# Layer 2 as seven block products before the mixing, and another order of the first gathers, in a four-layer graph network on one core

## The chip, the cores and the metric

The kernel runs on one core of one Trainium2 chip. Times are device microseconds (us) of one launch. Every ratio to the kernel before is between executions on the same chip in the same call; where a run is compared with the changed kernel or with another run, the two come from different calls, and between these the median of the kernel before went from 3187.1 to 3191.3 us. A ratio is the mean time of one kernel's fast runs over the mean of the other's of the same rounds, so it is not quite the ratio of the medians that are quoted. The profile is one execution, with times of each engine's instructions: PE is TensorE (matmul), DVE VectorE, ACT ScalarE, POOL GpSimd, SP SyncE. "Clock" is the share of full speed that TensorE's throttle granted.

## The reference

Input x is 128 batches of 128 nodes by 256 features, fp32; adj is a sparse 128 by 128 matrix. Four graph layers follow each other, each with a residual and a layer normalization:

```python
x = layernorm(x + attention_over_edges(x))          # layer 0: gathers, segment softmax, scatter
h = relu(Wt @ (x @ W1)); h = relu(Wt @ (h @ W2))    # layer 1, Wt = adj * adj
x = layernorm(x + Wt @ (h @ W3))                    #   widths 256, 512, 1024, 256
h = einsum('bjf,kfo->kbjo', x, W)                   # layer 2: three products 256 -> 256
x = layernorm(x + diag(adj) @ h[0] + triu(adj, 1) @ h[1] + tril(adj, -1) @ h[2] + bias)
x = layernorm(x + batchnorm2(relu(batchnorm1(A_hat @ x @ W1.T)) @ W2.T))   # layer 3 [cut]
```

Layer 2 may mix the nodes first and multiply by W afterwards, or the other way round. Mixing only acts on the nodes and W only on the features, so the results agree.

## The kernel before

A "quad" is four batches; 32 quads pass through a software pipeline. One iteration works on layer 2 and 3 of quad a = k-1, layer 1's second product of c = k, layer 1's start of b = k+1, the attention of e = k+2 and the queries of g = k+3. The schedule is written by hand: the program sets the order of each engine's work. The big products (layer 0's values, layer 1's first and second, layer 3's hidden) already use Strassen's scheme in Winograd's form: seven block products instead of eight, with sums of blocks on VectorE.

Layer 2 of one quad mixed each batch first (split_t holds the two triangles) and then made six matmuls of 256 columns per batch:

```python
def mix(i):                                   # [cut: allocation]
    for dc in range(DC):
        nc.tensor.matmul(pm[:, dc]..., s.xr[:, i, dc * P:(dc + 1) * P], split_t..., start=True, stop=True)
    nc.scalar.copy(ms[:, 1:3]..., pm)
    for dc in range(DC):
        nc.tensor.transpose(pt[:, dc, :], s.xr[:, i, dc * P:(dc + 1) * P], ident)
    nc.vector.tensor_mul(ms[:, 0], pt, diag_bc...)
def prod(i):
    for n3, (t, dc) in enumerate((t, dc) for t in range(3) for dc in range(DC)):
        nc.tensor.matmul(po[:, i % 2, :], mss[i][:, t, dc, :], l2w[:, t, dc, :],
                         start=(n3 == 0), stop=(n3 == 3 * DC - 1))
    if i % 2:
        nc.vector.tensor_add(xj, s.xb[:, i - 1:i + 1, :], po)     # residual; layer_norm(xj) later
```

One stretch is `second`, layer 1's second product of quad c. It has fourteen places at which other work can be hung in (`after(i)` runs what the schedule put at place i):

```python
product(y, 0, "A11", B11); keep(p1, 0, "p1"); after(0)
product(y, 1, "A11", B11); keep(p1, 1, "p1"); after(1)
product(x, 0, "A12", B21); total(0, 0, 0, x, p1); after(2)
product(z, 0, "S1", T1);   after(3)
product(y, 0, "S2", T2);   keep(u2, 0, "u2"); after(4)   # keep: ScalarE copies the bank
product(y, 1, "S2", T2);   keep(u2, 1, "u2"); relu(0, 0, 0); after(5)
product(x, 1, "A12", B21); total(1, 0, 0, x, p1); after(6)
product(y, 0, "S3", T3)    # accumulates into y[0]: only after the copy u2 has read it
# [cut: seven more products of this kind, up to after(13)]
```

The layer normalization takes statistics on VectorE (`ln_st`, `ln_mv`), a square root on ScalarE (`ln_sd`) and the rest on VectorE.

## Time and profile before

| | before |
|---|---|
| time, median of 3 (later 4) runs | 3188.79 us (3187.04 to 3189.34) |
| profiled span | 3186.6 us |
| TensorE, VectorE, ScalarE busy | 98%, 68%, 41% |
| period of one quad | 86.92 us |
| granted TensorE clock, whole span | 0.992 |

The prediction below shows the lines behind these numbers. One view it tells only in a sum is the list of what TensorE waited for (engine, what it wanted, who released it and where: total us, times, longest). The largest entries of the kernel before are:

```profile
PE py L443 <- ACT adc L429: 8.8, 1, 8.8
PE pt L1372 <- ACT agg L1214: 7.6, 4, 3.3
```

One happens once, the other four times. No entry happens once per quad: in the steady part there is no wait to remove.

### The profile page before, as it was taken

How to read it: one execution, taken by the hardware profiler on the slowest of the kernel's cores; microseconds unless marked ns; L12 is line 12 of the kernel's file. 1: busy time of each engine (PE TensorE's matmuls, PEld its weight loads, DVE VectorE, ACT ScalarE, POOL GpSimd, SP SyncE). 2: the span in 40 equal slices, each digit the busy share in tenths (PEclk: the TensorE clock that was granted, in tenths of full speed). 3: DMA queues.
4: the chain of work that ended last, by engine and by line, in shares of the span. 5: the costliest groups of instructions: out<-in, count | busy, mean ns of one | idle time of the engine just before them, and what ended most of it. 6: DMA issues, size and time to landing. Idle time of an engine off the chain costs nothing. (4 is left out here: it accounts for less than half of the span.)

```text
span 3186.6 us, 40910 instructions
## 1 busy us (share of the span) xinstructions
PE 3119.4 (98%) x15651; PEld 2574.5 (81%) x15651; DVE 2162.4 (68%) x4209; ACT 1311.9 (41%) x2359; POOL 649.2 (20%) x533
## 2 busy tenths in 40 slices
PE   7899999999999999999999999999999999999997
PEld 3788888888888888888888888888888888874444
DVE  6676666666767676666666767676666666438888
ACT  3344333334433434333334433433333333326668
POOL 3211222212211211222212211211222211001135
PEclk8899999999999999999999999999999999999999
DMA  7422333333333322333333333323333321005457
GB/s 210 132 73 81 100 107 100 107 92 102 107 95 98 100 86 80 100 106 100 106 90 103 107 91 102 98 86 82 100 106 100 105 84 51 21 27 193 175 199 266
DMA packets 117459, 340.12 MB, mean 107 GB/s; under 512 B 14864, under 2 KB 51600, under 8 KB 108944
## 3 DMA queue, kind: packets, MB, share of 16 engines
q0 software_dynamic: 44400, 147.35, 19.0%
q1 hardware_dynamic: 71104, 189.23, 16.4%
q8 instruction: 124, 2.03, 0.3%
q10 hardware_dynamic: 1760, 0.92, 0.1%
q14 instruction: 71, 0.58, 0.1%
HBM read 252.00 MB, written 85.46 MB: 106 GB/s over the span
## 5 line engine op out<-in xcount | busy, mean ns | idle before, releaser
L643 PE MATMUL p<-w,h 128*128 128x256 f32 x2048 | 464.7, 380 | 0.0
L562 PE MATMUL ph<-m,w 128*128 128x256 f32 x2048 | 463.0, 379 | 0.0
L643 PEld LDWEIGHTS p<-w,h 128*128 128x128 f32 x2048 | 389.8, 190 | 67.0 <-issue 8.3
L562 PEld LDWEIGHTS ph<-m,w 128*128 128x128 f32 x2048 | 386.8, 190 | 51.4
L331 POOL DMA_INDIRECT zs<-qd,src_idx x122 | 118.3, 970 | 1407.8 <-DMA qd<-qt 829.0
L562 PE MATMUL ph<-m,w_s 128*128 128x256 f32 x1536 | 354.4, 380 | 0.0
L693 PE MATMUL po<-l2w,ms 128*128 128x256 f32 x1536 | 347.5, 379 | 1.2 <-DVE ms L685 1.2
L562 PEld LDWEIGHTS ph<-m,w_s 128*128 128x128 f32 x1536 | 292.9, 191 | 40.2
L693 PEld LDWEIGHTS po<-l2w,ms 128*128 128x128 f32 x1536 | 284.4, 190 | 36.2 <-DVE ms L685 1.5
L113 ACT ACTIVATE ln_sd<-ln_mv,eps 128x2 f32<-128x2 f32 x192 | 56.2, 293 | 499.5 <-DVE ln_mv L108 499.5
L331 POOL DMA_INDIRECT zs<-qd,dst_idx x122 | 207.6, 1701 | 244.1 <-DMA zs<-qd,src_idx 236.2
L414 POOL DMA_INDIRECT attd<-at,att_idx x128 | 127.8, 998 | 300.6 <-DMA attd<-at,att_idx 239.3
L569 ACT COPY u<-ph 128x512 f32<-128x512 f32 x128 | 75.0, 586 | 247.6 <-PE ph L562 247.6
L575 DVE TENSOR_TENSOR h<-ph,u 128x512 f32<-128x512 f32 x128 | 88.2, 689 | 109.7 <-ACT u L569 58.1
L366 DVE TENSOR_TENSOR zs<-zs,a_bc 128x1024 f32<-128x1024 f32 x125 | 153.1, 1225 | 4.3
L367 DVE TENSOR_REDUCE scores<-zs 128x16 f32<-128x1024 f32 x125 | 152.5, 1220 | 4.3
L681 ACT COPY ms<-pm 128x512 f32<-128x512 f32 x128 | 71.2, 581 | 200.0 <-PE pm L679 200.0
L364 DVE SCALAR_TENSOR_TENSOR zs<-zs 128x1024 f32<-128x1024 f32 x125 | 152.1, 1217 | 1.3 <-DMA zs<-qd,dst_idx 1.3
L504 DVE TENSOR_TENSOR h<-z,adc 128x512 f32<-128x512 f32 x62 | 41.8, 674 | 156.5 <-ACT adc L498 156.5
L106 DVE BATCH_NORM_STATS2 ln_st<-xr 128x6 f32<-128x256 f32 x384 | 144.2, 418 | 5.5
L121 DVE TENSOR_SCALAR xr<-xr,ln_mv,ln_rs 128x256 f32<-128x256 f32 x384 | 142.6, 414 | 6.9
L667 POOL TENSOR_TENSOR xb<-xr,bias 128x512 f32<-128x512 f32 x64 | 81.5, 1273 | 298.3 <-DVE xr L121 159.3
(304 smaller groups left out, 5701.7 us busy)
## 6 DMA issues: line engine op xcount, KB each, us to landing
ad<-attd SPq DMA_DIRECT2D x32, 1024.0 KB, 4.8
zd<-z SPq DMA_DIRECT2D x31, 1024.0 KB, 7.4
zl<-zd SPq DMA_DIRECT2D x62, 512.0 KB, 3.5
xr<-in_x_dram SPq DMA_DIRECT2D x32, 512.0 KB, 5.9
x3d<-xr SPq DMA_DIRECT2D x32, 512.0 KB, 2.9
x3l<-x3d SPq DMA_DIRECT2D x32, 512.0 KB, 5.1
out_dram<-x3l POOLq DMA_DIRECT2D x31, 512.0 KB, 6.0
qd<-qt SPq DMA_DIRECT2D x30, 512.0 KB, 2.6
```

The lines of the kernel that those rows point to most:

```text
L106: nc.vector.bn_stats(st[:, i, :], r[:, i, :])
L121: nc.vector.tensor_scalar(r[:, i, :], r[:, i, :], mv[:, i, 0:1], rs[:, i:i + 1], op0=ALU.subtract, op1=ALU.mult)
L331: nc.gpsimd.indirect_dma_start(out=s.z[c], out_offset=None, in_=s.qd, in_offset=bass.IndirectOffsetOnAxis(ap=idx[:, c:c + 1], axis=0), com ...
L364: nc.vector.scalar_tensor_tensor(z, z, SLOPE, z, op0=ALU.mult, op1=ALU.max)
L366: nc.vector.tensor_mul(z3, z3, a_bc.unsqueeze(1).to_broadcast([P, QB, D]))
L367: nc.vector.reduce_sum(s.es[:, c, :], z.rearrange("p (r d) -> p r d", d=DH), axis=AX.X)
L414: nc.gpsimd.indirect_dma_start(out=ad, out_offset=bass.IndirectOffsetOnAxis(ap=att_idx[:, c:c + 1], axis=0), in_=s.at[:, c, :], in_offset= ...
L562: nc.tensor.matmul(bank[g][:, i].rearrange("p b n -> p (b n)"), wa[:, c, f:f + P], s.m2[:, blk_b, c].rearrange("p b n -> p (b n)"), start= ...
L575: nc.vector.tensor_add(block(g, row, col), bank[g], kept_[g])
L643: nc.tensor.matmul(p3[:, t * D:(t + 1) * D], s.h2[f // 2][:, f % 2, j + t, :], w3_sb[:, f, :], start=(f == 0), stop=(f == K2 - 1))
L667: nc.gpsimd.tensor_add(s.xb[:, j:j + 2, :], xj, bias.unsqueeze(1).to_broadcast([P, 2, D]))
L693: nc.tensor.matmul(po[:, i % 2, :], mss[i][:, t, dc, :], l2w[:, t, dc, :], start=(n3 == 0), stop=(n3 == 3 * DC - 1))
```

## The change

Layer 2 takes two batches as the two row blocks of one 2 x 2 block product: the transposed x of the pair times the three matrices W side by side (768 columns, in two halves of 384). Seven block products replace eight. Then split_t mixes the products of both batches in two matmuls of 512 columns, and the diagonal is applied on VectorE. The old fine interleaving is given up: the twelve products of a quad come in one run, and the two pairs' mixing and normalization are hung into `second`. The core of the diff, cut (the old `stage_e` is the code shown above):

```diff
-        def stage_e(k):                       # [cut: mix, prod]
+        def layer2(k, b):                     # [cut: buffers]
+            def head(p):                      # two transposes per batch, copy, four sums on VectorE
+                ...
+                def mm(bank, i, j, new):
+                    nc.tensor.matmul(bank[:, :half], a[i], layer2.blocks[j], start=new, stop=True, ...)
+                def part(bank, i):            # ScalarE keeps a partial sum
+                    ...
+                def out(row, col, bank, kept_):
+                    to = g[p][:, row, col * half:(col + 1) * half]
+                    if kept_ is None:
+                        nc.scalar.copy(to, bank[:, :half])
+                    else:
+                        nc.vector.tensor_add(to, bank[:, :half], kept_)
+                return Seven(mm, part, out)
+            def mix(p):
+                nc.vector.scalar_tensor_tensor(xb, g[p][:, :, :D], diag_col, xb, op0=ALU.mult, op1=ALU.add)
+                for i in range(2):
+                    nc.tensor.matmul(po, split_t[:, i, :], g[p][:, :, (i + 1) * D:(i + 2) * D], ...)
+                nc.vector.tensor_add(xj, xb, po)
+                layer_norm(wk, xj)
+            u = head(0)
+            mix2(b, 0); mix2(b, 1)            # layer 1's mixing of the next quad
+            v = head(1)
+            mix2(b, 2); mix2(b, 3)
+            run(u.p1, u.p2, u.p5, u.p6, v.p1, v.p2, u.p7, v.p5, v.p6, u.p4, u.p3, v.p7)
+            yield
+            v.p4()
+            yield
+            v.p3()
             mix(0)
+            yield
             mix(1)
@@ iteration
+                for i in (0, 1, 3):
+                    between[i].append(lambda: next(parts, None))
                 between[11].append(lambda: next(steps, None))
                 between[12] += [lambda: next(steps, None)] * 2
                 if has_e:
                     for c_, i in enumerate((0, 2, 7)):
                         between[i].append(lambda c_=c_: score(e, c_ + 1))
-                    for j, i in enumerate((1, 3, 8, 10)):
+                    for j, i in enumerate((5, 8, 9, 10)):
                         between[i].append(lambda j=j: by_row(b, j))
@@ start: quad 1's gathers use the unsorted edge lists and come before quad 0's scatters
+            for t in range(2):
+                for c in range(NE):
+                    gather_one(1, t, c, cols_i[:, t, :])
-            for c in range(NE):
-                gather_one(1, 0, c)
-            scatter(0, lambda c: gather_one(1, 1, c))
+            scatter(0, False)
+            score(1, 0, ends[:, 3, :])        # [cut: later scores, spreading and sums moved likewise]
```

`score` is one chunk of the attention scores on VectorE, `by_row` spreads attention weights on ScalarE, `steps` are the parts of the softmax.

More of the change, by code (lines that the diff above doesn't have):

```diff
@@ L80, in gnn_stack @@
     bn1, bn2 = ctile([P, 3, K3], "bn1"), ctile([P, 3, DC], "bn2")
-    w2t = ctile([P, K3, D], "l3w2")
     sc1, sh1 = ctile([P, K3], "sc1"), ctile([P, K3], "sh1")
@@ L85, in gnn_stack @@
     zpool = ctx.enter_context(tc.tile_pool(name="zpool", bufs=1))
+    xpool = ctx.enter_context(tc.tile_pool(name="xpool", bufs=1))
     kept = {}
@@ L213, in gnn_stack @@
         split_t = ctile([P, 2, N], "split_t", pool=cst)
-        diag_bc = ctile([P, N], "diag_bc", pool=cst)
+        diag_col = ctile([P, 1], "diag_col", pool=cst)
         ahat_t = ctile([P, N], "ahat_t", pool=cst)
@@ L270, in weight_blocks @@
         def weight_blocks(w, t):
-            b = {f"B{c + 1}{h + 1}": w[:, c, h * 256:(h + 1) * 256] for c in range(2) for h in range(2)}
+            half = w.shape[2] // 2
+            b = {f"B{c + 1}{h + 1}": w[:, c, h * half:(h + 1) * half] for c in range(2) for h in range(2)}
             b.update(T1=b["B12"], T2=t[:, 0], T3=t[:, 1], T4=t[:, 2])
@@ L326, in z_buffer, with gather_one @@
             return ws.tile([P, QB * D], F32, tag="zs", name=f"zs{k}_{c}", bufs=NE - 1)
-        def gather_one(k, t, c):
+        def gather_one(k, t, c, idx=None):
             s = quads[k]
-            idx, op = ((src_idx, ALU.bypass), (dst_idx, ALU.add))[t]
+            idx = idx if idx is not None else (src_idx, dst_idx)[t]
+            op = (ALU.bypass, ALU.add)[t]
             nc.gpsimd.indirect_dma_start(out=s.z[c], out_offset=None, in_=s.qd,
@@ L333, in gather_one, with gather_last @@
                                          compute_op=op)
-        def gather_last(k, steps=range(2)):
-            if 0 in steps:
-                quads[k].z[NE - 1] = z_buffer(k, NE - 1)
-            for t in steps:
+        def gather_last(k):
+            quads[k].z[NE - 1] = z_buffer(k, NE - 1)
+            for t in range(2):
                 gather_one(k, t, NE - 1)
@@ L408, in attention, with scatter @@
             nc.vector.tensor_mul(s.at, rden, pa[:, :, :R])
-        def scatter(k, between=None):
+        def scatter(k, load=True):
             s = quads[k]
@@ L415, in scatter, with load_weights @@
                                              in_=s.at[:, c, :], in_offset=None)
-                if between:
-                    between(c)
+            if load:
+                load_weights(k)
+        def load_weights(k):
+            s = quads[k]
+            ad = att_dram[k % 2]
             s.ad = wk.tile([P, N * R], F32, tag="ad", name=f"ad{k}", bufs=1)
@@ L667, in third_norm @@
             nc.gpsimd.tensor_add(s.xb[:, j:j + 2, :], xj, bias.unsqueeze(1).to_broadcast([P, 2, D]))
-        def stage_e(k):
+        def layer2(k, b):
             s = quads[k]
-            mss, po, pt = {}, None, None
-            def mix(i):
-                nonlocal pt
-                ms = wk.tile([P, 3 * DC * N], F32, tag="ms", name="ms").rearrange("p (k c n) -> p k c n", k=3, c=DC)
-                pm = ps("pm3").rearrange("p (c k n) -> p c k n", c=DC, k=2)
-                for dc in range(DC):
-                    nc.tensor.matmul(pm[:, dc].rearrange("p k n -> p (k n)"), s.xr[:, i, dc * P:(dc + 1) * P],
-                                     split_t.rearrange("p k n -> p (k n)"), start=True, stop=True)
-                nc.scalar.copy(ms[:, 1:3].rearrange("p k c n -> p c k n"), pm)
-                pt = ps("pt3")[:, :DC * N].rearrange("p (c n) -> p c n", c=DC)
-                for dc in range(DC):
-                    nc.tensor.transpose(pt[:, dc, :], s.xr[:, i, dc * P:(dc + 1) * P], ident)
-                nc.vector.tensor_mul(ms[:, 0], pt, diag_bc.unsqueeze(1).to_broadcast([P, DC, N]))
-                mss[i] = ms
-            def prod(i):
-                nonlocal po
-                if i % 2 == 0:
-                    po = ps("po2").rearrange("p (b d) -> p b d", d=D)
-                for n3, (t, dc) in enumerate((t, dc) for t in range(3) for dc in range(DC)):
-                    nc.tensor.matmul(po[:, i % 2, :], mss[i][:, t, dc, :], l2w[:, t, dc, :],
-                                     start=(n3 == 0), stop=(n3 == 3 * DC - 1))
-                if i % 2:
-                    xj = s.xr[:, i - 1:i + 1, :]
-                    nc.vector.tensor_add(xj, s.xb[:, i - 1:i + 1, :], po)
@@ new lines, in layer2 @@
+            adc = adc_tile()
+            g = [wk.tile([P, 2, 3 * D], F32, tag="ms", name="g", bufs=1),
+                 adc[:, :6 * D].rearrange("p (t f) -> p t f", t=2)]
+            sums = [adc[:, 6 * D:], None]
+            half = 3 * D // 2
+            def head(p):
+                pt = ps("pt3").rearrange("p (t c n) -> p t c n", t=2, c=DC)
+                for t in range(2):
+                    for c in range(DC):
+                        nc.tensor.transpose(pt[:, t, c, :], s.xr[:, 2 * p + t, c * P:(c + 1) * P], ident)
+                xt = temp("x2t").rearrange("p (t c n) -> p t c n", t=2, c=DC)
+                nc.scalar.copy(xt, pt)
+                room = sums[p] if p == 0 else temp("x2s")
+                a = {f"A{t + 1}{c + 1}": xt[:, t, c, :] for t in range(2) for c in range(DC)}
+                for i in range(4):
+                    a[f"S{i + 1}"] = room[:, i * N:(i + 1) * N]
+                sums_a(a, a)
+                keep = {}
+                def mm(bank, i, j, new):
+                    nc.tensor.matmul(bank[:, :half], a[i], layer2.blocks[j], start=new, stop=True,
+                                     skip_group_check=True)
+                def part(bank, i):
+                    if i < 2:
+                        keep[i] = temp("x2k")
+                    to = keep[i % 2][:, :half]
+                    nc.scalar.copy(to, bank[:, :half])
+                    return to
+                def out(row, col, bank, kept_):
+                    to = g[p][:, row, col * half:(col + 1) * half]
+                    if kept_ is None:
+                        nc.scalar.copy(to, bank[:, :half])
+                    else:
+                        nc.vector.tensor_add(to, bank[:, :half], kept_)
+                return Seven(mm, part, out)
@@ new lines, in mix @@
+            def mix(p):
+                xb = s.xb[:, 2 * p:2 * p + 2, :]
+                nc.vector.scalar_tensor_tensor(xb, g[p][:, :, :D], diag_col, xb, op0=ALU.mult, op1=ALU.add)
+                po = ps("po2").rearrange("p (t d) -> p t d", d=D)
+                for i in range(2):
+                    nc.tensor.matmul(po, split_t[:, i, :], g[p][:, :, (i + 1) * D:(i + 2) * D],
+                                     start=(i == 0), stop=(i == 1))
+                xj = s.xr[:, 2 * p:2 * p + 2, :]
+                nc.vector.tensor_add(xj, xb, po)
+                layer_norm(wk, xj)
@@ L699, in stage_e @@
+            u = head(0)
+            if b is not None:
+                mix2(b, 0)
+                mix2(b, 1)
+            v = head(1)
+            if b is not None:
+                mix2(b, 2)
+                mix2(b, 3)
+            run(u.p1, u.p2, u.p5, u.p6, v.p1, v.p2, u.p7, v.p5, v.p6, u.p4, u.p3, v.p7)
[3 more added lines that the diff above has]
+            v.p3()
             mix(0)
+            yield
             mix(1)
-            yield
-            prod(0)
-            yield
@@ L704, in stage_e @@
-            mix(2)
-            prod(1)
-            yield
-            mix(3)
-            layer_norm(wk, s.xr[:, 0:2, :])
-            prod(2)
-            yield
-            prod(3)
-            layer_norm(wk, s.xr[:, 2:4, :])
             nc.sync.dma_start(x3_dram[k], s.xr.rearrange("p b d -> p (b d)"))
@@ L717, in stage_f @@
             s = quads[k]
-            wide = [wk.tile([P, 3 * DC * N], F32, tag="ms", name="ag") for _ in range(DC)]
-            ag = [w[:, :QB * N] for w in wide]
-            s.spare = [w[:, QB * N:] for w in wide]
+            wide = wk.tile([P, DC, 3 * D], F32, tag="ms", name="ag", bufs=1)
+            ag = [wide[:, i, :QB * N] for i in range(DC)]
+            s.spare = [wide[:, i, QB * N:] for i in range(DC)]
             pas = [ps("pa") for _ in range(DC)]
@@ L796, in gnn_stack @@
         w3_sb = ctile([P, K2, D], "w3", pool=cst2)
-        l2w = ctile([P, 3, DC, D], "l2w", pool=cst2)
+        l2w = ctile([P, DC, 3 * D], "l2w", pool=cst2)
+        l2w_s = ctile([P, 3, 3 * D // 2], "l2w_s", pool=cst2)
         bias = ctile([P, D], "bias", pool=cst2)
@@ L823, in iteration @@
             parts = quads[a].layer2
-            for _ in range(3):
-                next(parts, None)
             if has_e:
@@ L828, in iteration @@
                 gather_last(e)
-            for _ in parts:
-                pass
+            if not has_c:
+                for _ in parts:
+                    pass
             steps = softmax_parts(e) if has_e else iter(())
@@ L839, in iteration @@
                 if has_b:
-                    for j, i in enumerate((1, 3, 8, 10)):
+                    for j, i in enumerate((5, 8, 9, 10)):
                         between[i].append(lambda j=j: by_row(b, j))
                 if has_g:
-                    between[11].append(lambda: values_in(g, quads[g].xg))
+                    between[13].append(lambda: values_in(g, quads[g].xg))
                 second(c, between)
             if has_g and g + 1 < NQ:
-                quads[g + 1].xg = load_x(g + 1, "xg", 1, ws)
+                quads[g + 1].xg = load_x(g + 1, "xg", 1, xpool)
+            elif has_g:
+                kept["w2t"] = xpool.tile([P, K3, D], F32, tag="xg", name="l3w2", bufs=1)
+                nc.sync.dma_start(kept["w2t"], l3_w2_t.rearrange("(c p) f -> p c f", p=P))
             if has_c:
@@ L894, in iteration @@
                 third_norm(c, 2)
-                quads[c].layer2 = stage_e(c)
+                quads[c].layer2 = layer2(c, None)
                 next(quads[c].layer2)
@@ L913, in iteration @@
             third_norm(c, 2)
-            quads[c].layer2 = stage_e(c)
+            quads[c].layer2 = layer2(c, b)
             next(quads[c].layer2)
-            for i in range(QB):
-                mix2(b, i)
         def iteration_0():
@@ L922, in iteration_0 @@
             between = {i: [] for i in range(14)}
-            between[0] = [lambda: score(2, 0), lambda: gather_last(2, range(1))]
-            between[1] = [lambda: next(quads[1].steps), lambda: next(quads[1].steps, None)]
-            between[3] = [lambda: attention(1), lambda: scatter(1), lambda: gather_last(2, range(1, 2))]
+            between[0] = [lambda: score(2, 0), lambda: gather_last(2)]
             for c, i in ((1, 2), (2, 5)):
                 between[i].append(lambda c=c: score(2, c))
+            for j, i in enumerate((8, 9, 10, 11)):
+                between[i].append(lambda j=j: by_row(1, j))
+            between[9].append(lambda: score(2, NE - 1))
             second(0, between)
@@ L932, in iteration_0 @@
             first_seven.blocks = weight_blocks(w1_sb, w1_s)
-            for j in range(QB):
-                by_row(1, j, nc.vector.tensor_copy if j % 2 else None)
             next(rest)
             aggregate(1)
-            score(2, NE - 1)
             next(rest)
@@ L965, in iteration_0 @@
             third_norm(0, 2)
-            quads[0].layer2 = stage_e(0)
+            layer2.blocks = weight_blocks(l2w, l2w_s)
+            quads[0].layer2 = layer2(0, 1)
             next(quads[0].layer2)
-            for i in range(QB):
-                mix2(1, i)
             queries.blocks = weight_blocks(wqv, wqv_s)
@@ L1025, in start @@
             nc.sync.dma_start(att_dram[1][:N * N, :].rearrange("(t s) r -> t (s r)", s=N), zero)
-            quads[3].xg = load_x(3, "xg", 1, ws)
+            quads[3].xg = load_x(3, "xg", 1, xpool)
             nc.sync.dma_start(w2_sb, w2.rearrange("(c p) f -> p c f", p=P))
             nc.sync.dma_start(w3_sb, w3.rearrange("(c p) f -> p c f", p=P))
-            nc.sync.dma_start(l2w, l2_w.rearrange("k (c p) f -> p k c f", p=P))
+            for c in range(DC):
+                nc.sync.dma_start(l2w[:, c, :].rearrange("p (k f) -> p k f", k=3),
+                                  l2_w[:, c * P:(c + 1) * P, :].rearrange("k p f -> p k f"))
             nc.sync.dma_start(bias, bass.AP(tensor=l2_bias.tensor, offset=l2_bias.offset, ap=[[0, P], [1, D]]))
             nc.sync.dma_start(l3w1, l3_w1_t.rearrange("(c p) f -> p c f", p=P))
-            nc.sync.dma_start(w2t, l3_w2_t.rearrange("(c p) f -> p c f", p=P))
             for t, vecs in ((bn1, (l3_b1, l3_g1, l3_be1)), (bn2, (l3_b2, l3_g2, l3_be2))):
@@ L1082, in start @@
                 values(1, 2 * c + 1, nc.scalar.copy)
+            quads[1].z = {0: z2[:, 1, :], 1: z_buffer(1, 1), 2: z_buffer(1, 2), 3: z2[:, 0, :]}
             nc.vector.tensor_tensor(keep_f[:, 1:], src_row[:R, 1:], src_row[:R, :E - 1], op=ALU.is_equal)
@@ L1091, in start @@
                 score(0, c, ends[:, 3, :])
+            for t in range(2):
+                for c in range(NE):
+                    gather_one(1, t, c, cols_i[:, t, :])
             sorted_scores(0, perm, range(NE - 1))
@@ L1100, in start @@
                 nc.vector.tensor_copy(to, pc[:, :, t])
-            quads[1].z = {0: z2[:, 1, :], 1: z_buffer(1, 1), 2: z_buffer(1, 2), 3: z2[:, 0, :]}
-            for c in range(NE):
-                gather_one(1, 0, c)
             for _ in steps:
@@ L1119, in start @@
             nc.vector.tensor_copy(adj_t, pr)
-            pr = ps("diag_ps")[:, :N]
-            nc.tensor.matmul(pr, ones, diag, start=True, stop=True)
+            nc.vector.reduce_sum(diag_col, diag, axis=AX.X)
             nc.vector.tensor_mul(wt_t, adj_t, adj_t)
@@ L1126, in start @@
                                     compare_op=ALU.is_gt, fill=0.0)
-            nc.vector.tensor_copy(diag_bc, pr)
             nc.vector.tensor_add(an, a_sb, ident)
@@ L1131, in start @@
             nc.vector.reduce_sum(sums[:, 1:2], diag, axis=AX.X)
-            second_sums()
             values(2, 2, nc.scalar.copy)
@@ L1140, in start @@
             values_in(3, quads[3].xg, nc.scalar.copy)
-            quads[4].xg = load_x(4, "xg", 1, ws)
-            score(1, 0)
+            quads[4].xg = load_x(4, "xg", 1, xpool)
+            load_weights(0)
+            score(1, 1, ends[:, 3, :])
             dinv = sums[:, 5:6]
@@ L1148, in start @@
             nc.tensor.transpose(pr, diag, ident)
-            score(1, 1)
             nc.vector.tensor_scalar(ahat_t, pr, dinv, None, op0=ALU.mult)
+            score(1, 2, ends[:, 3, :])
+            score(1, NE - 1, ends[:, 3, :])
             for i in range(1, QB):
@@ L1154, in start @@
                 by_row(0, j, nc.vector.tensor_copy if j % 2 else None)
+            sorted_scores(1, perm)
             aggregate(0)
             gather(2)
-            score(1, 2)
             stage_a(0)
-            score(1, NE - 1)
+            steps = softmax_parts(1)
+            for _ in range(5):
+                next(steps)
+            second_sums()
             mix1(0, 0)
@@ L1163, in start @@
             first(0, 1)
-            steps = softmax_parts(1)
-            next(steps)
+            for _ in steps:
+                pass
             for i in range(QB):
@@ L1168, in start @@
                     first(0, i + 1)
-                if i < 2:
-                    next(steps)
+                if i == 1:
+                    attention(1)
+                    scatter(1)
                 mix2(0, i)
-            next(steps)
-            next(steps)
-            quads[1].steps = steps
         with tc.manual_schedule(engines=None):
@@ L1180, in gnn_stack @@
                 iteration(k)
+    w2t = kept["w2t"]
     with ExitStack() as phase:
```

## The prediction

> **What bounds the kernel now.** I read the page first, then busy time by stretches, then one steady iteration of the timeline on TensorE, VectorE and ScalarE.
>
> ```profile
> PE 3119.4 (98%) x15651; PEld 2574.5 (81%) x15651; DVE 2162.4 (68%) x4209; ACT 1311.9 (41%) x2359; POOL 649.2 (20%) x533
> ```
> ```profile
> 1000.00:1086.90 86.90, 86.90 (x464) 75.83 (x463) 59.02 (x114) 33.86 (x60) 17.33 (x14) 1.00 0.34 98
> ```
> One quad of batches takes 86.9 us (the same matmul group starts at 1044.07 and again at 1130.99), and in this stretch TensorE (second column) never stops: it is the bound. VectorE has 27.9 us of slack per quad, ScalarE 53. Idle TensorE time, 67 us in all, lies in the first 320 us (29 us) and after 2640.
>
> ```profile
> 1041.90 1.03 PE L679 MATMUL pm<-split_t,xr 128*128 128x256 f32 x4
> ...
> 1044.07 3.74 PE L525 MATMUL pm<-wt_t,h 128*128 128x128 f32 x32
> 1047.64 2.76 PE L693 MATMUL po<-l2w,ms 128*128 128x256 f32 x12
> ...
> 1054.99 5.35 PE L693 MATMUL po<-l2w,ms 128*128 128x256 f32 x24
> ```
> Each fp32 matmul leaves two records: the last 24 are 12 matmuls and take 1060.17-1054.99 = 5.18 us up to the next group, so 0.432 us per 256 columns. A 384-column one should take 0.648, a 512-column one 0.864; a 128x128 transpose (one record) takes 0.108.
>
> ```profile
> 1057.71 1.22 DVE L364 SCALAR_TENSOR_TENSOR zs<-zs 128x1024 f32<-128x1024 f32 x1
> 1058.96 1.22 DVE L366 TENSOR_TENSOR zs<-zs,a_bc 128x1024 f32<-128x1024 f32 x1
> 1060.22 1.22 DVE L367 TENSOR_REDUCE scores<-zs 128x16 f32<-128x1024 f32 x1
> 1061.35 0.68 DVE L697 TENSOR_TENSOR xr<-xb,po 128x512 f32<-128x512 f32 x1
> 1062.07 0.75 DVE L106 BATCH_NORM_STATS2 ln_st<-xr 128x6 f32<-128x256 f32 x2
> 1062.74 0.30 DVE L108 BATCH_NORM_AGGREGATE ln_mv<-ln_st 128x2 f32<-128x6 f32 x2
> 1063.40 0.17 DVE L119 RECIPROCAL ln_rs<-ln_sd 128x2 f32<-128x2 f32 x1 [0.36 <-ACT ln_sd L113]
> 1063.60 0.73 DVE L121 TENSOR_SCALAR xr<-xr,ln_mv,ln_rs 128x256 f32<-128x256 f32 x2
> 1064.25 1.22 DVE L364 SCALAR_TENSOR_TENSOR zs<-zs 128x1024 f32<-128x1024 f32 x1
> ```
> This gives VectorE's real spacing: a chunk of scores 3.64 us (1057.71 to 1061.35), the residual addition 0.72, the normalization of two batches 2.18 including its trip to ScalarE for the root.
>
> ```profile
> 1042.95 0.63 ACT L505 ACTIVATE h<-h 128x512 f32<-128x512 f32 x1 [1.06 <-DVE h L504]
> ...
> 1063.07 0.30 ACT L113 ACTIVATE ln_sd<-ln_mv,eps 128x2 f32<-128x2 f32 x1 [6.25 <-DVE ln_mv L108]
> 1063.27 1.14 ACT L569 COPY p<-ph 128x512 f32<-128x512 f32 x2
> ```
> The second pair shows ScalarE standing at the root until VectorE has the statistics, while the copy behind it (its product left TensorE at about 1062.1) waits too. Here that costs nothing, since TensorE needs that bank only later.
>
> [...] The trace agrees on the half clock, but already after 2.36 us without a matmul (115.69 to 118.05; the clock is the third figure from the right):
>
> ```profile
> 116.00:118.00 2.00, 0.00 (x0) 0.00 (x0) 1.94 (x3) 0.00 (x0) 1.46 (x1) 1.00 0.00 0
> 118.00:120.00 2.00, 1.95 (x9) 1.66 (x10) 1.97 (x3) 0.00 (x0) 0.00 (x0) 0.77 0.82 270
> 120.00:122.00 2.00, 2.00 (x6) 1.58 (x5) 1.97 (x2) 0.44 (x1) 0.00 (x0) 0.50 0.00 0
> ```
> About 3.4 us run at half clock (back at 1.00 by 124), which loses 1.7 us. [...] 128 columns 0.29 us and 512 columns 0.69, as this trace has them, so 384 should be 0.56 (about 0.48 apart when independent).
>
> **The change, TensorE's work.** Out go 24 matmuls of 256 columns per quad (six per batch): 24 x 0.432 = 10.36 us. In come 14 of 384 (seven per pair): 14 x 0.648 = 9.07. Mixing stays (8 x 0.432 becomes 4 x 0.864), and so do 8 transposes. Saved: 1.29 us per quad, 41 us over 32 quads, 1.3%. That is all the arithmetic offers.
>
> **VectorE and ScalarE.** Out: four multiplications by the diagonal (4 x 0.42). In: eight sums of 128 columns (8 x 0.29), six bank additions of 384 (6 x 0.56), two diagonal updates (2 x 0.69): 7.0-1.7 = 5.4 us more on VectorE per quad. ScalarE gets about 2.6 more. In total both fit their slack; the order is what matters. I read it from the built program, matching each wait with the instruction that ends it, and count from t=0, the end of the last first-layer product (1041.90 above).
>
> Wait A. The first mix2 needs the hidden tile that is added on VectorE and rectified on ScalarE until 1043.58, t=1.68. Before, two mixes (2.17 us) stood in between; now only four transposes (0.43) and the two mix2 matmuls that don't need the tile (0.43). TensorE waits 0.9 us, with restarting 1.0, in 31 quads: +31 us.
>
> Wait B. Then TensorE: two mix2 and the second transposes to t=3.5, two more mix2 to 5.2, twelve products (7.8) to 13.0. The last product's copy leaves ScalarE at 13.65. From there VectorE runs one unbroken queue: bank addition 0.5, two late sums 1.3, scores 3.64, scores 3.64, last bank addition 0.45, diagonal update 0.7, residual 0.7, normalization 2.2, a total 0.6, scores 3.64, diagonal 0.7, residual 0.7, statistics of the second pair 1.0. Sum 19.8, so t=33.5. The second root is put into ScalarE's queue ahead of the copy u2 of layer 1's second product; root and copy end at t=34.3. The third product into that bank (S3 with T3) must wait for this copy. TensorE's own path from 13.0 to it is seven layer-1 products of 1.727 (eight records each at 0.216), two late products of 0.648 and four mix matmuls of 0.864: 12.1+1.3+3.5 = 16.9, t=29.9. So it waits 34.4-29.9 = 4.5 us (0.5 of it a little earlier, where the second pair's mix waits for VectorE). This needs three chunks of scores in flight, so it strikes iterations 1 to 29: 29 x 4.5 = +130 us. Before, the same stretch had one residual and normalization, no diagonal updates or bank additions, and layer 2's products finished first.
>
> Clock. A wait of 4 us exceeds the one of 2.36 us that halved the clock: 29 x 1.7 = +49 us, the least certain term.
>
> Start and tail. Before, ScalarE's spreading of quad 0's weights ended an 8.84 us TensorE wait at 83.23; quad 0's scatters alternated with quad 1's gathers (56.7, 62.2, 65.5, 69.8). With the gathers issued before them from the unsorted indices, scatters should follow 2.4 us apart (as at 126.43, 128.80, 131.18), but VectorE then has quad 1's scores before its share of the spreading. I estimate -8 us. In the last quad there is no mix2 to cover the second transposes' wait for their normalization: +3.
>
> Sum: 3188.8 - 41 + 31 + 130 + 49 + 3 - 8 = 3353 us. I put the point at 3345, as any slip in the VectorE chain would shorten Wait B.
>
> **Rivals.** (1) Pure TensorE arithmetic with everything hidden: 3189-41-8 = 3140, 1.5% faster. TensorE's 98% and the slack of VectorE speak for it; the two queues speak against it. (2) Only wait A: about 3170, within 2%. It needs the second root to come early or the copy not to stand behind it; the built order says otherwise. (3) Both waits but an undisturbed clock, because the rest of the time around is dense: 3304. (4) VectorE as a throughput bound: no, 59.0+5.4 us of 87.
>
> **Range and chances.** Wait B could be 3.5 to 5 us, and the clock loss 0 to 2.5 us, in 29 iterations; that gives 3275 to 3390. I widen it below, for a fault in the reading of the order: 3225 to 3395. Faster by over 2% needs 64 us, more than TensorE's saving and the start together: 0.04. Within 2% if wait B is mostly absent: 0.12. Slower: 0.84.
>
> **What would show it.** TensorE's matmul on layer 1's second-layer bank with long idle before it, released by ScalarE's copy u2, near 4 us for each of 29 iterations; ScalarE's u2 copy directly after the second root ln_sd, which waits for VectorE; 0.9 us before mix2, released by ScalarE's h; a period near 93 us; granted clock under 1.00 in mid slices; products of 384 columns 0.65 us apart. If the period is about 86 and TensorE stays at 98%, Wait B is wrong; if it is 91 with full clock, only the clock term is.

Passages that told rules and figures which no trace of this case shows are cut from the text on record. Its sum: 3188.8 - 41 (TensorE's work) + 31 (wait A) + 130 (wait B) + 49 (clock) + 3 (tail) - 8 (start) = 3353 us, and the point was put at 3345. What the argument needs stands on the trace of before. The copy behind a root starts 1.2 us after its product (1062.1 to 1063.27). What is measured is a half clock after 2.36 us without a matmul. The 0.56 us of a 384-column addition is an estimate between the 0.29 and 0.69 us of 128 and 512 columns in that trace, and its 0.48 takes off the 0.08 us by which two independent 512-column ones overlap there (0.69 long, 0.61 apart: 1040.05 and 1040.66). The trace of the changed kernel has 0.56 and 0.48 (1026.12 to 1026.60). The 0.1 us of restarting in wait A fits that trace: twelve records of `po<-l2w,ms` take 2.86 us after a wait of 1.25 (2843.32) and 2.76 without one (1047.64).

## The result, and the profile after

The changed kernel is correct and takes 3385.53 us, median of 4 runs (3384.30 to 3389.67), against 3188.81 for the kernel before in the same rounds: ratio 1.062, 95% interval 1.0602 to 1.0639. It is 6% slower.

The engines' line of the page after (busy us, share of the span, instructions):

```profile
PE 3167.5 (94%) x14760; PEld 2445.6 (72%) x14760; DVE 2335.9 (69%) x4598; ACT 1391.3 (41%) x2549; POOL 654.8 (19%) x533
```

TensorE has 891 fewer matmul records than before, and yet 48 us more busy time: it is slower while it works. Its idle time rose from 67 to 215 us. Two successive quads in the view of busy time by stretches (stretch, length; busy us of PE, PEld, DVE, ACT, POOL with instruction counts; clock; DMA share; GB/s):

```profile
1012.27:1105.50 93.23, 88.11 (x434) 71.64 (x433) 64.44 (x126) 36.31 (x66) 17.29 (x14) 0.98 0.33 93
1105.50:1199.98 94.48, 89.35 (x434) 72.60 (x433) 64.78 (x126) 36.29 (x66) 17.25 (x14) 0.96 0.31 88
```

A quad takes 93.2 and 94.5 us in turn, at a clock of 0.98 and 0.96, with VectorE busy for only 64 of them. The mean of the 27 periods from 261.55 to 2795.20 us is 93.84. TensorE's timeline in the first of the two (start, us, line, operation, records, in brackets the idle time before it and who ended it):

```profile
1014.00 1.61 PE L530 MATMUL pm<-wt_t,h 128*128 128x128 f32 x12 [0.68 <-ACT h L510]
...
1017.67 0.81 PE L700 MATMUL y<-l2w,x2t 128*128 128x384 f32 x2
1018.32 0.81 PE L700 MATMUL x<-l2w,x2t 128*128 128x384 f32 x2
...
1035.91 1.96 PE L724 MATMUL po<-adc,split_t 128*128 128x512 f32 x4 [0.42 <-DVE adc L715]
...
1041.16 1.89 PE L567 MATMUL ph<-m,w 128*128 128x256 f32 x8
1047.07 3.58 PE L567 MATMUL ph<-m,w 128*128 128x256 f32 x8 [4.02 <-ACT u L574]
```

The new products are 0.65 us apart (1017.67 to 1018.32). There are three waits: the mixing of layer 1's hidden tile h (L530), the mixing of layer 2's second pair (L724), and layer 1's second product, whose bank the copy u2 must have read (L567, u). The last product before the long one lasts 1.73 us, so by its spacing TensorE was free at 1042.89 and stood for 4.18 us (a wait in brackets is some 0.16 us shorter than the gap from start to start: the 384-column products above are listed with 0.81 us and start 0.65 apart). And the eight records after the wait take 3.58 instead of 1.89 us: half speed. The same three waits in the list of what TensorE waited for:

```profile
PE ph L567 <- ACT u L574: 115.8, 29, 4.4
PE pm L530 <- ACT h L510: 21.2, 31, 0.7
PE po L724 <- DVE adc L715: 15.4, 29, 3.6
```

Why the copy u was late is read in the timeline of all engines just before it:

```profile
1044.52 0.69 DVE L727 TENSOR_TENSOR xr<-xb,po 128x512 f32<-128x512 f32 x1
...
1045.91 0.30 DVE L108 BATCH_NORM_AGGREGATE ln_mv<-ln_st 128x2 f32<-128x6 f32 x2
1046.25 0.29 ACT L113 ACTIVATE ln_sd<-ln_mv,eps 128x2 f32<-128x2 f32 x1 [7.70 <-DVE ln_mv L108]
1046.45 1.05 ACT L574 COPY u<-ph 128x512 f32<-128x512 f32 x2
```

ScalarE stood 7.70 us at the second pair's root, with the copy that TensorE needed directly behind it. Last, stretches cut at the moments where the clock changes, after the wait of the first and of the second quad shown above (1047.07 and 1140.30 are the ends of the waits):

```profile
1047.30:1050.72 3.42, 3.42 (x9) 2.71 (x9) 0.81 (x2) 1.71 (x4) 0.00 (x0) 0.50 0.41 158
1050.72:1053.00 2.28, 2.28 (x12) 2.00 (x12) 1.69 (x2) 2.08 (x3) 0.00 (x0) 1.00 0.00 0
...
1139.46:1142.88 3.42, 2.58 (x6) 2.14 (x7) 1.50 (x4) 2.73 (x5) 0.00 (x0) 0.50 0.39 156
1142.88:1146.30 3.42, 3.42 (x9) 2.71 (x9) 1.57 (x2) 2.10 (x3) 0.00 (x0) 0.50 0.00 0
```

In the first quad the clock is 0.50 for 3.42 us. In the second it drops 0.84 us before the wait ends, is 0.50 for 3.42 us, and stays so for another 3.42. Half clock during work costs half of it, as in the eight records above (3.58 us for 1.89): 3.42/2 = 1.7 us in the one, (6.84 - 0.84)/2 = 3.0 in the other.

### The profile page after: what moved, and what is told of

The parts are those of the page before. It is cut to its first block, busy times and chain, and to the rows that moved or that the text cites. A ratio compares the mean times of both kernels' runs of the same rounds, so it can differ in the third digit from the quotient of the medians.

```text
span 3382.6 us, 39848 instructions
## 1 busy us (share of the span) xinstructions
PE 3167.5 (94%) x14760; PEld 2445.6 (72%) x14760; DVE 2335.9 (69%) x4598; ACT 1391.3 (41%) x2549; POOL 654.8 (19%) x533
## 5 line engine op out<-in xcount | busy, mean ns | idle before, releaser
L567 PE MATMUL ph<-m,w 128*128 128x256 f32 x2048 | 528.6, 408 | 115.8 <-ACT u L574 115.8
L567 PEld LDWEIGHTS ph<-m,w 128*128 128x128 f32 x2048 | 413.2, 204 | 216.5 <-ACT u L574 127.4
L333 POOL DMA_INDIRECT zs<-qd,src_idx x120 | 137.2, 1143 | 1564.5 <-DMA qd<-qt 1005.7
L567 PE MATMUL ph<-m,w_s 128*128 128x256 f32 x1536 | 375.0, 392 | 0.0
L567 PEld LDWEIGHTS ph<-m,w_s 128*128 128x128 f32 x1536 | 308.7, 201 | 61.5 <-issue 15.4
L333 POOL DMA_INDIRECT zs<-qd,dst_idx x120 | 187.9, 1566 | 254.3 <-DMA zs<-qd,src_idx 246.0
L530 PE MATMUL pm<-wt_t,h 128*128 128x128 f32 x1024 | 133.4, 278 | 21.2 <-ACT h L510 21.2
L707 ACT COPY x2k<-y 128x384 f32<-128x384 f32 x192 | 91.8, 478 | 139.1 <-PE y L700 111.7
L584 ACT ACTIVATE h<-h 128x512 f32<-128x512 f32 x192 | 121.5, 633 | 53.2 <-DVE h L580 53.2
L530 PEld LDWEIGHTS pm<-wt_t,h 128*128 128x128 f32 x1024 | 122.0, 192 | 28.1 <-ACT h L510 27.1
```

What stands on the lines that cost most here:

```text
L333: nc.gpsimd.indirect_dma_start(out=s.z[c], out_offset=None, in_=s.qd, in_offset=bass.IndirectOffsetOnAxis(ap=idx[:, c:c + 1], axis=0), com ...
L530: nc.tensor.matmul(pm[:, c // 2, c % 2, :], s.h1[i, c], wt_t, start=True, stop=True)
L567: nc.tensor.matmul(bank[g][:, i].rearrange("p b n -> p (b n)"), wa[:, c, f:f + P], s.m2[:, blk_b, c].rearrange("p b n -> p (b n)"), start= ...
L584: nc.scalar.activation(h, h if src_ is None else src_, AF.Relu)
L707: nc.scalar.copy(to, bank[:, :half])
```

## The experiments

All ten kernels gave a correct result. They were run at other times. "Period" is the distance of the starts of successive quads' first layer-2 matmuls, steady in each run unless said. Edits are against the changed kernel unless said.

### Two ways to get the copy u2 out earlier

The theory: u2 is late because it stands in ScalarE's queue behind a root that waits for VectorE's queue. The first run changes ScalarE's order and leaves VectorE's (on TensorE the second pair's two mixing matmuls come two products later with it).

```diff
-                for i in (0, 1, 3):
+                for i in (0, 1, 5):
                     between[i].append(lambda: next(parts, None))
```

> Only the place of the second pair's mixing and normalization changes: it comes after the block additions and copies of layer 1's second layer that follow its fifth step, so that the copy u2 stands in ScalarE's queue ahead of the second root and not behind it. VectorE's amount of work is unchanged. Theory (u2 is late because of its place behind the root, and the wait also halves TensorE's clock): the 4.2 us wait of the bank of layer 1's second layer and the 2.6 us of clock after it go, 29 x 6.8 = 197 us, so 3385 - 197 = 3188 us, up to 3230 if the later transposes of the scores now wait (my reading of the order says about 1 us a quad). Rival A (VectorE has too much work in this stretch, so another wait of the same size takes the place): 3340 to 3390. Rival B (the wait is for a bank to be read by others than ScalarE): no change, 3385.

Measured: 3245.13 us (3243.70 to 3247.82), against 3187.13 before; ratio 1.0182 (1.0165 to 1.0199). Period 88.84 us. Of the 197 us that I expected back, 140 came. The list of TensorE's waits:

```profile
PE pe L382 <- DVE scores L372: 26.4, 29, 0.9
...
PE ph L567 <- ACT u L574: 17.8, 29, 3.3
```

The wait for u2 is down to 0.5 us in the steady quads (3.3 is the first one), and the clock is whole (1.00 over the quad from 1058.40 us). But the transpose of the scores now waits 0.9 us. I had expected about 1 us a quad of such waits; with the ideal period found below (85.56) and the wait at the hidden tile (0.95, below) it is 88.84 - 85.56 - 0.95 = 2.3.

The second run changes VectorE's order and leaves ScalarE's.

```diff
-                    for c_, i in enumerate((0, 2, 7)):
+                    for c_, i in enumerate((0, 3, 7)):
                         between[i].append(lambda c_=c_: score(e, c_ + 1))
```

> Only VectorE's order changes: the third chunk of scores (3.64 us) comes after the second pair's normalization instead of before it. ScalarE's order stays, u2 is still behind the second root. Theory (the root comes late because of the chain on VectorE): the wait for u2 falls from 4.2 to about 0.5 us and is then too short to halve the clock, 29 x (3.7 + 2.6) = 183 us, so 3202 us, up to 3235 with 1 us a quad at the scores' transposes. Rival (ScalarE's own queue, or work on ScalarE before the root, makes u2 late): still about 4 us of wait and 3370 to 3390.

Measured: 3241.66 us (3241.33 to 3244.42), ratio 1.0168 (1.0151 to 1.0185), a little worse than my upper figure. Its list of TensorE's waits:

```profile
PE pm L530 <- ACT h L510: 21.1, 31, 0.7
PE po L724 <- DVE adc L715: 15.4, 29, 3.6
PE ph L567 <- ACT u L574: 10.7, 28, 0.4
PE pe L382 <- DVE scores L372: 9.7, 28, 0.4
```

So either order, alone, removes the long wait and the clock loss (the clock is 1.00 over the quads from 969.56 us in the first run and from 968.80 in the second); ScalarE's order and VectorE's queue were both needed for it. The rival that something else held the bank falls. The two runs have other waits and yet the same period, 88.83 and 88.84 us. I read this as VectorE's queue setting both: the scores' transposes need all of its work of this stretch, in whatever order. The traces agree: in both runs these transposes start 40.4 us after the start of their quad and have waited for VectorE's scores. The later runs, which move them, bear it out.

### Is the rest really the clock?

Here TensorE gets something to do in the wait: eight matmuls into a bank that has been read already, put before the product that waits for u2.

```diff
             total(0, 0, 0, x, p1)
+            s.fill = x[0]
             after(2)
@@ iteration
+                def filler():
+                    for _ in range(8):
+                        nc.tensor.matmul(quads[c].fill[:, 0]..., second.blocks["A11"][:, 0, :P],
+                                         quads[c].m2[:, 0, 0]..., start=True, stop=True, skip_group_check=True)
+                if has_e:
+                    between[6].append(filler)
```

> Eight matmuls of 128 columns (3.46 us at full clock) into a bank that has been read already are put on TensorE just before the product that waits for u2. They compute nothing that is used. The wait for u2 thus stays, but TensorE works through nearly all of it. Theory (2.6 us a quad are the half clock after the idle time): the work after the wait runs at full clock, 29 x 2.6 = 75 us come back, 3310 us. My own recorded term of 1.7 us would give 3336. Rival (the 2.6 us come from something else, such as a longer wait or contention for memory): 3385, or more where the additional work delays.

(The text calls them matmuls of 128 columns; they have 256, which is what its 3.46 us are computed from.) Measured: 3323.58 us (3322.85 to 3326.19), ratio 1.0428 (1.0410 to 1.0445), 62 us less than the changed kernel, though TensorE does more. One quad, and the product after the wait:

```profile
995.22:1086.78 91.56, 89.87 (x451) 73.49 (x450) 64.65 (x126) 36.35 (x66) 17.32 (x14) 1.00 0.31 88
```
```profile
1030.02 1.99 PE L567 MATMUL ph<-m,w 128*128 128x256 f32 x8 [0.58 <-ACT u L574]
```

The clock is 1.00, the eight records take 1.99 us, the period does not alternate any more and is 91.55. The product after the wait starts 34.8 us after the start of its quad, just as in the changed kernel: the copy u2 comes as late as before, and only the idle time is filled. The clock therefore costs 93.84 - 91.55 = 2.29 us a quad. My figure for this run (3310) took 2.6, which I had got by subtracting the waits that I could see; some 0.3 us of that were not clock.

Then half the filling, four matmuls (`range(4)`), so that TensorE stands about 2.3 us:

> As the run with eight additional matmuls before the wait for u2, but with four: TensorE then works 1.7 us of the 4.2 and idles about 2.4 us, as long as the idle time after which the kernel before had half its clock (2.36 us). Theory (such a time is enough): the clock still halves in all or part of the quads and the time lies between 3345 and 3385 us. Rival [...]: full clock, and 3323 us as with eight.

Measured: 3345.21 us (3339.54 to 3348.12), ratio 1.0486 (1.0469 to 1.0504), at the edge of the theory's range. In the trace there are 28 such waits after the first one, 26 of 2.30 us and two of 2.65. The clock halves after 10 of them (the nine in the steady part give a period of 93.2) and holds after the others (91.55). One quad of each kind, in stretches of 2 us around the end of the wait (at 1039.63 and at 946.40), each with the idle time of 2.30 us before it:

```profile
1039.00:1041.00 2.00, 1.37 (x6) 1.25 (x7) 1.50 (x4) 2.00 (x5) 0.00 (x0) 1.00 0.05 20
```
```profile
946.00:948.00 2.00, 1.60 (x4) 1.34 (x5) 1.41 (x4) 2.00 (x4) 0.00 (x0) 0.64 0.16 63
948.00:950.00 2.00, 2.00 (x6) 1.55 (x6) 0.00 (x0) 0.31 (x1) 0.00 (x0) 0.51 0.49 199
```

The same wait of 2.30 us halves the clock or does not, quad by quad. So the length of the wait alone does not decide it.

The traces show what else matters. In each of the twelve, every change of the clock, the first and last us of the span left out, lies within 0.02 us of one grid with a step of 3.413 us (71 changes in the trace of the changed kernel, 19 in that of before). Here are the same two quads again, cut at this grid:

```profile
943.16:946.57 3.41, 1.11 (x6) 0.66 (x5) 2.87 (x9) 0.99 (x3) 0.00 (x0) 1.00 0.00 0
946.57:949.98 3.41, 3.41 (x9) 2.70 (x10) 0.87 (x2) 1.74 (x3) 0.00 (x0) 0.50 0.38 154
...
1035.32:1038.73 3.41, 2.01 (x10) 1.43 (x8) 3.27 (x7) 0.00 (x0) 0.00 (x0) 1.00 0.00 0
1038.73:1042.14 3.41, 2.51 (x12) 2.23 (x13) 1.55 (x5) 3.22 (x6) 0.00 (x0) 1.00 0.37 149
```

In the first quad the whole wait lies in one step of the grid, and the next step runs at half clock. In the second it is split into 1.4 and 0.9 us, and the clock holds. Laid on the grid in the same way, the ten waits that halved the clock had 2.1 us or more in one step, and the other eighteen 2.0 or less. These two figures hold for this dense stretch: at the end of the changed kernel's trace, where the work is sparser, the clock halves after a wait of 1.61 us (3322.12 to 3323.74).

### The wait at the hidden tile

mix2 of the tiles that are ready (2 and 3) is put first, with the evictions in the old order, before the second pair's transposes.

```diff
             u = head(0)
-                mix2(b, 0)
-                mix2(b, 1)
+                for i in (2, 3, 0, 1):
+                    mix2_mm(b, i, pms[i])
+                mix2_out(b, 0, pms[0])
+                mix2_out(b, 1, pms[1])
             v = head(1)
-                mix2(b, 2)
-                mix2(b, 3)
+                mix2_out(b, 2, pms[2])
+                mix2_out(b, 3, pms[3])
```

> The mixing of layer 1's hidden tiles comes before the transposes of the second pair and takes the two tiles that are ready first; only the last two wait for the tile that VectorE and ScalarE just made. Theory (0.86 us a quad of TensorE time are lost to that tile and everything after it moves along): 31 x 0.86 = 27 us, 3358 us. Rival (the wait for u2 is set by something that does not move with TensorE, so the gain is given back there): 3385, with the wait for u2 longer by 0.9 us.

Measured: 3338.64 us (3338.37 to 3340.25), ratio 1.0472 (1.0455 to 1.0490). The wait is gone, but the gain is 47 us, more than either expectation: the period falls by 1.68 us to 92.16 and no longer alternates, and the clock over a quad is 0.98 in each:

```profile
1002.10:1094.27 92.17, 87.72 (x435) 71.48 (x433) 64.36 (x126) 36.02 (x66) 17.30 (x14) 0.98 0.31 88
```

To see whether the surplus is clock, both edits together:

> The reordered mixing of the hidden tiles and the eight additional matmuls together. The reordering alone gained 47 us, where the wait it takes away is 31 x 0.96 = 30 us. Theory (the other 17 us were TensorE's clock, which came back after one window of half clock in every quad instead of alternately one and two): with the clock kept up by the additional matmuls the reordering gains only 30 us, 3324 - 30 = 3294 us. Rival (the reordering takes away more waiting than I count): 3324 - 47 = 3277 us.

Measured: 3297.42 us (3293.72 to 3299.72), ratio 1.0338 (1.0321 to 1.0355). This is 26 us less than with the filling alone, though measured in another call; by the period it is 91.55 - 90.60 = 0.95 us a quad, or 29 us in 31 quads, and the profiled start was 3 us later. The theory's 30 holds: with the clock whole, the hidden tile's wait costs 0.95 us; the other 0.7 us of the gain were clock.

### The start alone

The kernel before, with only the new order of gathers, scores and spreading of the first quads; layer 2 as before (a long diff of `start` and the first iteration, cut to its core).

```diff
+            for t in range(2):
+                for c in range(NE):
+                    gather_one(1, t, c, cols_i[:, t, :])
-            scatter(0, lambda c: gather_one(1, 1, c))
+            scatter(0, False)
```

> The kernel before with nothing but the new order of the first quads' gathers, scores and spreading; layer 2 as before. Theory (the start gains what the trace of the changed kernel shows at its first layer-2 products, 6.3 us): 3187 - 6 = 3181 us, with the first layer-2 group some 6 us earlier. My recorded term was -8: 3179. Rival (the start's gain is waited for later in the first quad, where something else is bound): 3187.

Measured: 3184.90 us (3184.60 to 3186.76) against 3188.66, ratio 0.9991 (0.9974 to 1.0007). The interval holds no gain as well. In its trace the first layer-2 matmuls start at 169.47 us instead of 172.70, and this 3.2 us stays to the end of the span (3183.5 against 3186.6). In the changed kernel's trace they started at 166.43. Over the eleven profiled runs with the new start they begin at 165.6 to 166.5 five times and at 169.1 to 170.2 six times; what decides between the two I did not find. (The six late ones have a stretch at half clock that begins between 59.9 and 63.1 us, and none of the five early ones has it; whether that is the cause is not shown.) So by these traces the start gains 3 or 6 us.

### A version that beats both

The pieces together: the two orders above (second pair at place 5, hidden tile), the third chunk of scores at place 9, the spreading at places 8, 9, 10, 12, and the softmax's scans behind later products.

```diff
-                for i in (0, 1, 3):
+                for i in (0, 1, 5):
-                between[11].append(lambda: next(steps, None))
-                between[12] += [lambda: next(steps, None)] * 2
+                between[13].append(lambda: next(steps, None))     # transposes of the scores, four copies
-                    for c_, i in enumerate((0, 2, 7)):
+                    for c_, i in enumerate((0, 2, 9)):
-                    for j, i in enumerate((5, 8, 9, 10)):
+                    for j, i in enumerate((8, 9, 10, 12)):
 # [cut: the hidden tile's order, and next(steps) moved behind layer 3's products]
```

> Everything that the first runs point to at once: the second pair's normalization behind u2, the hidden tile's mixing without its wait, the third chunk of scores later and with it the transposes that take all four chunks, the spreading of the weights later, and the scans of the softmax moved behind later products to make room. Theory (the new order of work was the whole loss, and TensorE's arithmetic gain is real): the period falls from 88.8 to about 85.6 us (86.9 of before minus 1.3), so 3187 - 41 - 6 (start) = 3140 us, up to 3165 with small waits that I did not see; faster than both kernels. Rival (VectorE's chain of this stretch only moves on and holds something behind, such as the softmax and with it the scatter of the weights): 3200 to 3300.

Measured: 3171.87 us (3168.56 to 3176.97) against 3188.66, ratio 0.9945 (0.9928 to 0.9961), period 86.22: between theory and rival. One wait per quad was left:

```profile
PE pe L382 <- DVE scores L372: 12.7, 28, 0.7
```

So this step was moved behind layer 3's aggregation:

```diff
-                between[13].append(lambda: next(steps, None))
             stage_f(a)
+            next(steps, None)
```

> As the run with everything at once, but the transposes that wait 0.44 us for the last chunk of scores stand behind 1.9 us of aggregation products. Theory (this wait was all that kept the period at 86.22 us): 86.92 - 1.29 = 85.63 us a quad, 28 x 0.6 = 17 us less than that run, and 2 us at the last quads where the aggregation's copies came behind the scores' copies: 3172 - 19 = 3153 us, 1.1% under before. Rival (the scores' chain then holds the softmax, the scatter and the spreading behind it): 3165 to 3185.

Measured: 3175.60 us (3166.46 to 3176.59) against 3191.32, ratio 0.9944 (0.9930 to 0.9958). The period is 86.20, no better. The time lies in the rival's range, but the wait is another than the rival named:

```profile
PE y L289 <- ACT m L306: 10.8, 28, 0.4
```

The four copies of the scores now stood in ScalarE's queue ahead of a copy m that a query product waits for. It is the same pattern as u2 behind the root, with a tenth of the wait. One place later again (after that copy):

```diff
             stage_f(a)
-            next(steps, None)
@@
                 q.p1()
             next(steps, None)
             if has_g:
                 run(q.p5, q.p2, q.p6)
+            next(steps, None)
```

> As the last run, but the scores' transposes and their four copies on ScalarE come one product later, behind the copy m whose delay (0.37 us of wait, 0.57 from start to start) took the place of the wait for scores; the first scan on VectorE comes a step later too. Theory (ScalarE's order alone made that wait): 85.63 us a quad, 16 us less than the last two: about 3156 us. Rival (each place in this dense stretch has another copy that must not be late; the wait turns up again as 0.3 to 0.6 us elsewhere): 3168 to 3176, as the last two.

Measured: 3152.69 us (3151.21 to 3156.22) against 3190.51, ratio 0.9877 (0.9861 to 0.9894): 1.2% faster than the kernel before (and, by the medians, 7% under the changed one). A quad of it:

```profile
1032.16:1117.73 85.57, 85.57 (x435) 70.62 (x434) 64.28 (x126) 35.56 (x66) 16.83 (x14) 1.00 0.36 99
```

TensorE is busy for the whole of the quad at full clock, and no steady wait is left in its list. The period is 85.56 us, 1.36 under before.

## Why the prediction was right or wrong

The direction and the mechanism were right, and 3385.5 lies within the range, 40 us above the point and 32 above the sum. Two terms, wait B and the clock, were too small by 16 and 17 us, in the same direction, so no error hid another. The measured column of the table is a chain of differences between runs and so adds up by construction. Wait A and the clock each rest on two runs that differ in that alone. TensorE's work and wait B rest on the last version, which has another order of scores, spreading and softmax as well; they are read from it because its quad has no wait left. Per quad:

| term | predicted, us | measured, us | from |
|---|---|---|---|
| TensorE's work | -1.29 | -1.36 | 86.92 to 85.56, the version without waits |
| wait A, hidden tile | +1.0 | +0.95 | filling with and without the reordering: 91.55 to 90.60 |
| wait B, u2 (and 0.5 before it) | +4.5 | +5.04 | 90.60 to 85.56 |
| clock | +1.7 | +2.29 | with and without filling: 93.84 to 91.55 |
| sum | +5.9 | +6.92 | 86.92 to 93.84 |

**TensorE's work: right.** The 384-column products are 0.65 us apart, as scaled from the 0.432 of 256 columns.

**Wait A: right**, 0.95 us in 31 quads.

**Wait B: right in mechanism, 0.5 us too small.** VectorE's queue from the bank addition behind the last product's copy to the second pair's statistics was counted as 19.8 us; in the trace it runs from 1026.12 to 1046.21, 20.1 us. The wait of the product is 4.18 us from start to start and the second pair's mix waits 0.58, which gives 4.76; most of the remaining 0.3 us I put down to restarting: summed from start to start, and with the waits and the filling taken off, layer 1's second product takes 0.11 us more in the run with both edits than in the last version, layer 2's mixing of the second pair 0.08 and a query product 0.07. Over 29 quads the term is 16 us larger than predicted. Both orders that shorten the chain, on ScalarE or on VectorE, removed the wait, so "the order is what matters" is shown. Lowering the point from the sum "as any slip in the VectorE chain would shorten Wait B" was wrong: nothing slipped.

**Clock: right in mechanism, the term that was mis-sized most.** "29 x 1.7 = +49 us, the least certain term" became 29 x 2.29 = 66 us. What failed is the reading of one instance in the trace of before as the price of each: one stretch of 3.4 us at half clock. The clock changes on a grid of 3.413 us (above), and in the steady quads of the changed kernel a stretch at half clock lasts one step of it or two (3.41 or 6.83 us). When the clock drops well before the wait ends (0.84 us in the quad shown, 0.8 to 1.1 in the fourteen of this kind), the grid step in which work resumes does not bring it back, and a second one passes at half speed; where at most 0.6 us of that step is idle (all quads of the run with wait A removed), the clock is back after the one. The long kind happened in every second quad: the mean of 1.7 and 3.0 is 2.35, near the 2.29 measured by filling. With wait A removed, each quad pays only the shorter kind (92.16 - 90.60 = 1.56 us). Two of the changed kernel's quads take 187.71 us, which is 55.0 steps of 3.413, and the reordered kernel's 92.16 is 27.0 of them, as if the loop locked to the grid; no run varied this on purpose, so it stays an observation.

**Start and tail: small and about right.** The start gained 6.3 us in the changed kernel's trace and 3.2 by itself, not 8. In the last quad, the distance from its first layer-2 matmul to the end is 0.8 us longer than before, not 3.

**Rivals.** Rival 3 (both waits, clock undisturbed, 3304) is what the filling makes: 3324, the waits being larger. Rival 1 (all hidden, 3140) is what the last version nearly reaches: 3153. So TensorE's saving was real from the beginning, and the order of two queues hid it. What I had no term for is what came behind: once u2 was early, the scores' transposes waited, then a copy m. Each was visible only after the wait before it had gone.

## What to carry to other kernels

When a change moves work between engines, follow the queue of each engine, in the order the program gave it, up to the instruction that the bound engine waits for; 64 us of work in 94 did not keep VectorE from holding up TensorE. An item that waits long (here a root that waited 7.70 us) must not stand ahead of a copy that releases a bank of the bound engine. Price a wait on TensorE of the lengths that halved the clock here (2.30 us in about a third of the cases, 4.02 us in every steady one) with the half clock behind it, in its bad case too, and when it can't be removed, try filling it with work.
